# A graph-network layer with a mixture of experts: the general path at the end is entered by a two-way switch, announced ahead, in place of a conditional

## The chip, the cores and the metric

The kernel runs on one core of a Trainium2 chip. A core has five engines that run their own instruction streams: TensorE (PE; its weight loads are shown as PEld), VectorE (DVE), ScalarE (ACT), GpSimd (POOL) and SyncE (SP). DVE, ACT and PE compute; SP here only issues transfers (DMAs) and waits. Engines wait for one another, and for the landing of transfers, by semaphores. The metric is the device time of one execution in microseconds (us), as the median of several runs.

## The reference

There are 625 nodes with 1024 features and 20,000 edges of two types. Cut to what matters:

```python
def reference(x, src, dst, edge_type_2, ...):
    x = x + gnn(_layernorm(x))            # 1. graph layer
    x = x + ffn(_layernorm(x))            # 2. mixture of experts
    return x

def gnn(h):                               # NUM_REL = 2, D_FF = 286
    n = ln_weight * h * rsqrt(mean(h * h) + 1e-6)
    y = n @ W_root + conv_bias
    for r in range(2):                    # mean over the edges of type r into a node
        w = (edge_type == r)
        sums = segment_sum(n[src] @ W_rel[r] * w[:, None], dst)
        cnt = segment_sum(w, dst)
        y = y + sums / maximum(cnt, 1)[:, None]
    return h + elu(y) @ wo_weight

def ffn(x):                               # 8 experts, 2 of them for each token; 2 shared ones
    shared = mean over s of (gelu(x @ sW1[s] + sb1[s]) @ sW2[s] + sb2[s])
    gates = x @ rW + rb
    w = softmax of the two largest gates, zero elsewhere
    moe = sum over e of w[:, e] * (gelu(x @ W1[e] + b1[e]) @ W2[e] + b2[e])
    return shared + moe
```

## The kernel before

The program holds two complete versions of the computation. `sparse_kernel` is the fast one. It counts edges in windows and routes tokens to the experts in slots of fixed number, so it holds only if every edge fell into its window and the routed tokens fit into the slots. It notes in `flag`, one integer in on-chip memory, whether either was violated. `dense_kernel` is the general one, which holds for any input. `gnn_ffn_kernel` runs `sparse_kernel` first, then loads the flag into a register of each engine (L1467) and, if it is above zero, runs `dense_kernel` as well, which writes the output anew (`tc.If`, L1468). With the inputs measured here the flag says that nothing was violated, so the general path is jumped over: its instructions stand in each engine's stream between the branch and the common end.

The flag is made up in two places. `check` (L697, L698) counts the edges found; `slots`, near 160 us, adds the excess of the routing and writes `flag` (L1256, L1257).

The work of `sparse_kernel` runs over five tiles of 125 nodes. First come the graph layer's projections and aggregations, then the shared experts' first matrices (L1115), the routing (`route`, `slots`), the gathered tokens through the experts' two matrices (L1337, L1395), and a scatter of the results to a table in memory by GpSimd (L1403; the handles are kept in the list `sent`). The table is read back by transfers of SP into the tiles `gs`.

Last is the output loop, over the five tiles `d`. For each tile TensorE multiplies the shared experts' hidden values with their second matrices into `p_o` (L1450) and adds the biases (L1452), in pieces of 512 columns (for the last tile 512, 256 and 256). VectorE adds each piece to `x1` by `add` (L1426), in an order fixed by hand with `tc.issue_after`, which queues an instruction behind another on its engine without waiting for the other's end. `store` (L1434) sends a finished tile, or for the last tile a finished piece, to the output: SP sends the first 112 rows, ScalarE's queue the last 13.

After the branch each engine raises the semaphores that the general path would have raised (its instructions are put down to L1468), and SP waits there for the landing of the stores. Then the tile context ends (L1497): SP waits for all, and a barrier over the engines closes the program.

`mybir.EngineType` names the engines, `nc.values_load` loads a value from on-chip memory into a register, and `PARTS` holds the two row ranges of `store`.

## Time and profile before

| | us |
|---|---|
| runs | 310.52, 310.69, 311.41 |
| median | 310.69 |
| profiled execution | 312.2 |
| its span, first to last instruction | 310.0 |
| TensorE busy in the span | 297.6 |
| last matmul ends | 303.55 |
| last addition ends | 304.01 |

The profile comes from one execution. Its times count from the first instruction of the program. An engine name with a `q` (SPq, PEldq) is the engine's sequencer: register, branch, semaphore and DMA-issuing instructions, which are not counted as busy time. The granted clock of TensorE was 0.998 of full speed.

In a source view each line holds the kernel's line, the engine, the operation, the tiles it writes and reads, a count, the shortest, median and longest duration in ns, and the first and last start in us. In the DMA view a queue has its packets, megabytes and share of the 16 DMA engines' time; the queues with the kind `instruction` bring the engines' own code, and q1 and q10 carry the data transfers of SP and ScalarE.

### The profile page before, as it was taken

What the parts mean: (1) busy time and instruction counts of PE and PEld (TensorE: products, weight loads), DVE (VectorE), ACT (ScalarE), POOL (GpSimd) and SP (SyncE); (2) the same over time, 40 slices, a digit from 0 to 9 for tenths busy, and PEclk for the clock granted to TensorE, in tenths of its full rate; (3) what the DMA queues carried; (4) which work ended last, traced back from release to release, by engine and by line L of the source; (5) the groups of instructions that cost most, each with busy time, mean ns of one, the idle gap of its engine ahead of it and who ended that gap; (6) DMA issues with size and microseconds to landing.
All of it is one profiled execution on the core that took longest, in us unless ns stands there. A gap on an engine that the chain in (4) does not pass through costs nothing.

```text
span 310.0 us, 4844 instructions
## 1 busy us (share of the span) xinstructions
PE 297.6 (96%) x1693; PEld 200.9 (65%) x1693; DVE 180.7 (58%) x541; ACT 110.1 (36%) x248; POOL 46.7 (15%) x98
## 2 busy tenths in 40 slices
PE   8799999999999999999999999999999999999991
PEld 7577777887888763456777798877854334444451
DVE  4899999977879676873895032122214211256920
ACT  3456123432436245333424145456459421000000
POOL 9600000000000012431112032120002232200000
PEclk9999999999999999999999999999999999999999
DMA  7999900000000499999999843421047555579351
GB/s 235 306 317 401 406 31 0 3 0 2 0 0 2 126 345 303 388 390 388 319 342 408 349 147 127 137 76 62 0 135 305 218 209 200 201 285 374 154 161 45
DMA packets 27409, 61.18 MB, mean 197 GB/s; under 512 B 2175, under 2 KB 16006, under 8 KB 27374
## 3 DMA queue, kind: packets, MB, share of 16 engines
q1 hardware_dynamic: 21806, 43.77, 39.8%
q0 software_dynamic: 5280, 16.69, 14.9%
q10 hardware_dynamic: 294, 0.35, 0.5%
q8 instruction: 16, 0.26, 0.4%
q14 instruction: 13, 0.11, 0.1%
HBM read 42.76 MB, written 18.81 MB: 199 GB/s over the span
## 4 chain that ended last, share of the span: by engine, by line
PE 78%; DVE 14%; DMA 3%; ACT 1%; issue 1%; SPq 1%; ACTq 0%
PE p_h L1337 12%; PE p_yj L1395 12%; PE p_pr L880 11%; PE p_o L1450 11%; PE p_sh L1115 10%; PE p_y L941 5%; PE p_agg L898 4%; DMA xh<-in_x_dram 3%; PE p_x L1318 3%; DVE ohk L850 2%; PE p_t L787 2%; DVE ohs L847 2%; DVE ohs L846 2%; PE cnt L859 2%; PE p_y L945 1%; DVE ct L808 1%
## 5 line engine op out<-in xcount | busy, mean ns | idle before, releaser
L880 PE MATMUL p_pr<-wg,nT 128*125 128x286 f32 x240 | 61.9, 408 | 0.0
L880 PEld LDWEIGHTS p_pr<-wg,nT 128*125 128x125 f32 x240 | 43.4, 187 | 11.9 <-ACT nT L793 0.4
L1337 PE MATMUL p_h<-w1a,xsT 128*128 (+2 forms) x176 | 40.0, 380 | 0.0
L1395 PE MATMUL p_yj<-w2a,hjT 128*128 (+2 forms) x88 | 38.6, 594 | 0.0
L1450 PE MATMUL p_o<-sw,shT 128*125 128x512 f32 (+1 forms) x88 | 36.1, 553 | 0.0
L1115 PE MATMUL p_sh<-h2T,sw 128*128 128x313 f32 (+1 forms) x128 | 35.2, 428 | 0.0
L1337 PEld LDWEIGHTS p_h<-w1a,xsT 128*128 128x128 f32 (+2 forms) x176 | 28.7, 168 | 7.4 <-issue 0.5
L1115 PEld LDWEIGHTS p_sh<-h2T,sw 128*128 128x128 f32 x128 | 23.7, 189 | 8.6 <-issue 0.2
L1395 PEld LDWEIGHTS p_yj<-w2a,hjT 128*128 128x128 f32 (+2 forms) x88 | 14.4, 168 | 22.4 <-issue 22.1
L1450 PEld LDWEIGHTS p_o<-sw,shT 128*125 128x125 f32 x88 | 16.4, 187 | 16.9 <-issue 16.2
L1399 DVE COPY ys<-p_yj 128x512 f32<-128x512 f32 x15 | 10.4, 692 | 28.7 <-PE p_yj L1395 27.1
L1341 DVE COPY hj<-p_h 128x256 f32<-128x256 f32 x11 | 4.7, 425 | 31.1 <-PE p_h L1337 31.1
L850 DVE TENSOR_TENSOR ohk<-iotk,cols 125x512 f16<-125x512 f16 (+4 forms) x49 | 22.3, 455 | 0.0
L846 DVE TENSOR_TENSOR ohs<-iota,cols 125x512 f16<-125x512 f16 (+3 forms) x49 | 18.2, 372 | 6.5 <-PE cnt L859 6.5
L898 PE MATMUL p_agg<-P,CT 125*125 125x287 bf16 x150 | 20.4, 286 | 0.2 <-DVE P L888 0.2
L955 POOL DMA_DIRECT2D x1d<-xh x10 | 5.3, 533 | 101.6 <-DVE xh L948 101.2
L859 PE MATMUL cnt<-ohk,ohs 125*128 125x128 f16 x223 | 17.9, 219 | 2.8 <-DVE ohs L847 2.8
L859 PEld LDWEIGHTS <-ohs 125*128 125x128 f16 x223 | 14.6, 98 | 7.8 <-DVE ohs L847 4.2
L941 PE MATMUL p_y<-wo_t,eT 128*125 128x512 f32 x40 | 19.2, 603 | 0.0
L898 PEld LDWEIGHTS <-CT 125*125 125x125 bf16 x150 | 18.4, 136 | 0.1
L1403 POOL DMA_INDIRECT yt<-ys,row x11 | 10.8, 984 | 50.5 <-DVE ys L1399 50.5
L847 DVE TENSOR_TENSOR ohs<-ohs,cols 125x512 f16<-125x512 f16 (+3 forms) x49 | 18.1, 369 | 0.0
(295 smaller groups left out, 421.7 us busy)
## 6 DMA issues: line engine op xcount, KB each, us to landing
w1a<-in_L_ffn_W_dram SPq DMA_DIRECT2D x8, 1024.0 KB, 10.9
w2a<-in_L_ffn_W_dram SPq DMA_DIRECT2D x8, 1024.0 KB, 5.1
yt<-zero SPq DMA_DIRECT2D x2, 2560.0 KB
g<-yt SPq DMA_DIRECT2D x10, 512.0 KB, 7.7
sw<-in_L_ffn_sW_dram SPq DMA_DIRECT2D x4, 1024.0 KB, 5.5
x<-x1d SPq DMA_DIRECT2D x5, 500.0 KB
wg<-in_L_gnn_W_rel_dram SPq DMA_DIRECT2D x2, 1144.0 KB, 19.6
x1d<-xh POOLq DMA_DIRECT2D x5, 448.0 KB, 6.2
```

The source lines that it names most:

```text
L846: nc.vector.tensor_tensor(os, row[:, None].to_broadcast(shape), key, op=ALU.is_equal)
L847: nc.vector.tensor_tensor(os, os, both(VV_, 128)[1], op=ALU.mult)
L850: nc.vector.tensor_tensor(halves(oh_k[:, :g, :kn]), row[:, None].to_broadcast(shape), key, op=ALU.is_equal)
L859: nc.tensor.matmul(accs[w][:, : R * WD], oh_s[:, i, :], oh_k[:, i, (w - lo) * 128 : (w - lo + 1) * 128], start=first, stop=last)
L880: nc.tensor.matmul(p[:TP, :F], nT[:, k, m * TP : (m + 1) * TP], wg[:, k, r, :], start=(k == 0), stop=(k == KD - 1))
L898: nc.tensor.matmul(p[:TP, : F + 1], CT[:, m, at : at + TP], P[:, m, r, i], start=(m == 0 and i == 0), stop=(m == NT - 1 and i == 2))
L941: nc.tensor.matmul(ps[s][:TP, :], eT[:, k, :], wo_t[:, k, s * 512 : (s + 1) * 512], start=(k == 0), stop=False)
L1115: nc.tensor.matmul(p[:, : z - a], sw1[:, i, k, t * 128 : (t + 1) * 128], h2T[:, k, a:z], start=(k == 0), stop=(k == KD - 1))
L1337: nc.tensor.matmul(p[a:b, :H], xsT[j][:, k, a:b], w1m[j, a][:, 0, k, :] if a else w1a[:, bass.ds(e, 1), k, :], start=(k == 0), stop=(k == ...
L1395: made = nc.tensor.matmul(p[a:b], hjT[:, j, k, a:b], w2m[j, a, k][:, at] if a else w2a[:, bass.ds(e, 1), k, at], start=(k == 0), stop=(k = ...
L1403: sent.append(nc.gpsimd.indirect_dma_start(out=yt, out_offset=bass.IndirectOffsetOnAxis(ap=row[:, j : j + 1], axis=0), in_=y, in_offset=No ...
L1450: nc.tensor.matmul(p[:TP, :n], shT[:, i, k, own], sw2[:, i, k, at], start=(i == 0 and k == 0), stop=False)
```

## The change

The conditional becomes a switch over two arms. The flag is turned round: it is now 1 where nothing was violated and 0 otherwise (one more operation on VectorE), so it can be the index of the switch. Arm 0 is the general path; arm 1, the usual one, is empty and stands last. Each engine reaches its arm by a jump to a computed place. The flag is loaded before the output loop's code rather than behind it. `near_end` puts an announcement of the coming jump, with the index, into one engine's stream behind a given instruction: for SP and ScalarE behind the store of the last tile but one, for GpSimd behind the last scatter, for TensorE behind the last matmul of the last tile's first piece, and for VectorE behind the addition before that piece's. A usual arm ends with a jump of its own to the common end.

```diff
@@ -44,6 +44,7 @@
 NQ = NJ - NM2
+ENG = mybir.EngineType
 YB = 1024
@@ -1254,7 +1255,8 @@
         nc.vector.tensor_copy(flagf[:, 1:2], over[:1, 3:4])
-        nc.vector.tensor_tensor(flag, flagf[:, 0:1], flagf[:, 1:2], op=ALU.add)
+        nc.vector.tensor_tensor(flagf[:, 0:1], flagf[:, 0:1], flagf[:, 1:2], op=ALU.add)
+        nc.vector.tensor_scalar(flag, flagf[:, 0:1], 0.5, None, op0=ALU.is_lt)
         return named
@@ -1431,8 +1433,18 @@
     def store(d, at):
         for g, eng in zip(PARTS, (nc.sync, nc.scalar)):
-            eng.dma_start(out[d * TP + g.start : d * TP + g.stop, at], x1[g, d, at])
-
+            put = eng.dma_start(out[d * TP + g.start : d * TP + g.stop, at], x1[g, d, at])
+            if d == NT - 2:
+                near_end(ENG.SP if eng is nc.sync else ENG.Activation, put)
+
+
+    ok = nc.values_load(flag, min_val=0, max_val=1)
+
+    def near_end(engine, inst):
+        with tc.issue_after(inst.ins):
+            tc.switch_hint({engine: ok}, 2, "sparse")
+
+    near_end(ENG.Pool, sent[-1])
     banks = 0
     for d in range(NT):
@@ -1449,7 +1461,10 @@
                         nc.tensor.matmul(p[:TP, :n], shT[:, i, k, own], sw2[:, i, k, at],
                                          start=(i == 0 and k == 0), stop=False)
-                nc.tensor.matmul(p[:TP, :n], wT[:, own], b23[:, at], start=False, stop=True)
+                done = nc.tensor.matmul(p[:TP, :n], wT[:, own], b23[:, at], start=False, stop=True)
+            if d == NT - 1 and at.start == 0:
+                near_end(ENG.PE, done)
+                near_end(ENG.DVE, added[-1])
             add(x1[:, d, at], p[:TP, :n], 1.0 / NS, x1[:, d, at])
@@ -1457,16 +1472,17 @@
         if d < NT - 1:
             store(d, slice(0, D))
+    return ok
 
 
 def gnn_ffn_kernel(tc, *args):
     nc = tc.nc
     with tc.tile_pool(name="flags", bufs=1) as flags:
         flag = flags.tile([1, 1], I32, name="flag")
-        sparse_kernel(tc, flag, *args)
-        off = nc.values_load(flag, min_val=0, max_val=EC * 4 + 1)
-        with tc.If(off > 0):
-            dense_kernel(tc, *args)
+        ok = sparse_kernel(tc, flag, *args)
+        for arm in tc.Switch(ok, 2, hint="sparse"):
+            if arm == 0:
+                dense_kernel(tc, *args)
```

## The prediction, made before the changed kernel ran

> **What bounds the kernel now.** I read the profile's page first, then the chain of waits from 285 us on, then the source views of the flag's load (L1467), of the branch (L1468) and of the end of the tile context (L1497), then SP's waits and the DMA view of the last microseconds, since the change touches little ahead of them.

> ```profile
> PE 297.6 (96%) x1693; PEld 200.9 (65%) x1693; DVE 180.7 (58%) x541; ACT 110.1 (36%) x248; POOL 46.7 (15%) x98
> ```
> ```profile
> 303.57 0.02 issue
> 303.59 0.42 DVE x L1426
> ```
> TensorE runs without a gap up to 303.55 us, and the chain of real work ends with the last addition of L1426 at 304.01. The span is 310.0, so 6 us follow in which no engine computes. Whatever the change is worth is worth it there, unless it opens a hole in TensorE's stream before 303.55.

> ```profile
> L1467 PEldq TENSOR_LOAD <-flag x1: 320/320/320, 299.7 to 299.7; - x1
> L1467 DVEq TENSOR_LOAD <-flag x1: 542/542/542, 303.6 to 303.6; - x1
> L1467 ACTq TENSOR_LOAD <-flag x1: 819/819/819, 304.4 to 304.4; - x1
> ...
> L1468 SPq EVENT_SEMAPHORE  x8: 17/17/17, 307.7 to 308.3; - x8
> L1468 PEldq COMPARE_BRANCH  x1: 4067/4067/4067, 300.2 to 300.2; - x1
> L1468 DVEq COMPARE_BRANCH  x1: 72/72/72, 304.2 to 304.2; - x1
> L1468 PEldq EVENT_SEMAPHORE  x1: 51/51/51, 304.3 to 304.3; - x1
> L1468 SPq COMPARE_BRANCH  x1: 53/53/53, 304.4 to 304.4; - x1
> L1468 ACTq COMPARE_BRANCH  x1: 54/54/54, 305.3 to 305.3; - x1
> L1468 ACTq EVENT_SEMAPHORE  x1: 17/17/17, 305.8 to 305.8; - x1
> L1468 DVEq EVENT_SEMAPHORE  x1: 21/21/21, 307.4 to 307.4; - x1
> ```
> ```profile
> L1497 SPq EVENT_SEMAPHORE  x14: 17/28/28, 308.3 to 309.9; - x14
> ```
> ```profile
> SPq L1468 <- SPq L1468: 3.4, 2, 3.2
> ```
> ```profile
> q1 hardware_dynamic: 132, 0.12, 8.8%
> q8 instruction: 1, 0.02, 1.9%
> q14 instruction: 3, 0.02, 1.5%
> ```
> Each engine jumps over the general path. ACT is at its next instruction 0.41 us after its branch (305.38 to 305.79), DVE only after 3.07 us (304.29 to 307.36), and PE's branch itself lasts 4.07 us: those two wait for code that isn't there. SP branches at 304.46 and does its first semaphore at 307.67, but not for code alone: in the trace's semaphore records the last updates of the two final stores come at 307.652 (ACT's store) and 307.822 us (SP's), and SP passes the two waits at 307.668 and 307.839, 16 ns later each. So the landing of the last store ends the kernel, and 2.1 us of semaphores and barrier follow it (307.84 to 309.95).

> That landing is late for one reason that the DMA records show. The store's packets start at 304.85, and all but one DMA engine's share is through by 305.54. Updates up to 305.983 make up all but three; the others are at 306.480, 307.652 and 307.822. The last share (seven packets of 1,024 bytes from SP, one from ACT) starts at 306.47, just as a 16,384-byte packet of the instruction queue q8 ends (304.953 to 306.488), and is slowed by an 8,192-byte packet of q14 (306.426 to 306.919). So the last store queues behind instruction fetches. The 16,384-byte one starts 0.67 us after PE came out of its branch at 304.28; another packet of the same size (301.874 to 302.807) lies inside PE's 4.07 us. I read them as PE's demand and the next stretch of code that it asks for on arrival.

> **The change part by part.** *Flag.* DVE gets one 1x1 operation more near 160 us. Its neighbours last 0.13 to 0.14 us (L1256, L1257). It stands ahead of the chain that makes `tok` (L1234, 160.71), and the first gather starts at 161.16 and is used by PE at 177; PE has shared-expert matmuls (L1115) until then. At nothing; 0.14 us if that cover were gone.

> *Loads of the flag.* Five TENSOR_LOADs remain, moved ahead of the output loop's end. ACT's 0.82 and DVE's 0.54 leave the tail, but ACT was done at 305.9 and DVE at 307.5, before SP's landing waits: no gain by themselves. On PE the load of 0.32 us and the announcement now stand 36 instructions (two groups of 8+1 matmuls with their weights) ahead of the end. PE's sequencer is that far ahead: its load ran at 299.73 while those 36 were still to execute, so 3.8 us of matmuls cover it. If they didn't, PE would lose 0.3 to 0.8 us.

> *Announcements.* Each is some register operations (SP's FUSED_REGOPS took 0.19 us) and one hint. On SP and ACT they stand behind the store of tile 3 (293.75 us); behind them waits the store of 296.97, so 2.8 us of idle queue cover them. On DVE they follow the addition that ends at 294.32, with 1.9 us idle. On POOL they follow the last scatter at 268, with the barrier 36 us away. What a hint fetches moves among transfers that nobody waits for.

> *Entry.* A compare-and-branch becomes a computed jump: say 0.2 to 0.5 us of register work on SP (once to twice its FUSED_REGOPS and a branch of 0.05). SP would arrive near 305.2 rather than 304.9, and the landing can't come before 305.98: hidden. If all announcements hold, PE jumps at about 301 and its follow-up packet of 16,384 bytes falls near 302, under the last matmuls, not on the last store. DVE has no demand fetch; its follow-up packet comes about 0.6 us after its arrival (0.59 in this trace, 307.36 to 307.94), near 305, as do SP's and ACT's. These are 8,192 bytes each (0.31 to 0.49 us), and one may stand ahead of one engine's share.

> *Landing.* Bounds: 305.98, the last update that nothing delayed (gain 1.84 us), and 307.82 as now (0). I take 306.48, the update that is 0.5 late at present, since one small packet in the way is what remains: gain 1.34 us.

> *Exit.* The usual arm holds SP's eight waits and then a jump to the common end, which follows the landing, so it counts in full. A taken branch whose code is there costs from its end to the next instruction 0.14 (POOL, 268.90 to 269.04) to 0.41 us (ACT), and itself 0.05. I take 0.28, the middle, as neither engine is SP. From below it can't be under 0.05, the branch itself. If the code isn't there it costs 3.07 (DVE), priced under the rivals. [...]

> *Sum.* The profiled execution took 312.2 us, 2.2 of them outside its span. 312.2 - 1.34 + 0.28 = 311.14. The median of the three runs is 310.69, 1.5 lower than the profiled one, so the same 1.06 less gives 309.63. The case's own range is a gain of 0.5 to 1.8 us: 308.9 to 310.2.

> [...]

> **The rivals.** *1, the store still waits (no change).* The follow-up packets of DVE, SP and ACT all come on arrival, now within 304.8 to 305.6, when the store's own packets flow. Three of 0.31 to 0.49 behind one another are 0.9 to 1.5 us on one DMA engine, against the 1.5 + 0.5 of now. For it: the trace already shows two such packets and a fetch on one share. Against: two updates were late by different amounts, so not all packets go one way. Then the gain is 0.3 to 0.9, less the exit's 0.28: 310.0 to 310.7.

> *2, the exit is not there (slower).* The usual arm is a small island behind the general path's block, and the common end lies beyond it. If SP's exit jump fetches its code, that stands behind the landing: 306.48 + 0.51 for eight semaphores (308.345 less 307.839) + 0.05 + 3.07 = 310.1, where now L1497 starts at 308.35: +1.8 us, 312.4. It decides if SP's step from the exit to L1497 exceeds 1.3 us; below that the earlier landing pays for it. For it: DVE and PE miss when they jump today. Against: ACT, POOL and SP seem to find theirs, and the end code is short.

> *3, the change doesn't do what it says.* The announcement is dropped or comes to nothing, and SP misses at the entry: 304.9 + 3.07 = 308.0, then 0.51 and the exit's 0.28, 308.8 where it is 308.35 now: +0.4 us, 311.1.

> **How the numbers follow.** Forecast 0.65, rival 1 0.12, rival 2 0.13, rival 3 0.10. A measurement of this kernel can tell about 0.3%, 0.93 us, from no change: bounds 309.76 and 311.62. The forecast's range lies for three quarters below 309.76 (its centre 0.13 below, the landing bounded at 305.98 above): 0.49 faster, 0.16 within. Rival 1 is within; rival 2 is slower; rival 3 is split, as its +0.4 would be 1 us if ACT or DVE lag too: 0.05 each. So faster 0.49, within 0.33, slower 0.18. The range 308.9 to 311.5 takes in the forecast, rival 1 and most of rival 3, and leaves out rival 2 and some of the edges. The forecast's own: 308.9 to 310.2.

> **What would show it.** Right: PE's jump ends before 303 and no instruction packet of 16,384 bytes lies between 304 and 307; DVE's step after its jump falls from 3.07 to under 0.5 us; SP's first landing wait ends by 306.5; its exit step is under 0.5; the rest from L1497 on stays at 1.6 us (308.35 to 309.95). Wrong: PE's last matmul later than 303.55 by more than 0.3; an SP landing wait still near 307.7; or more than 1.3 us between SP's last semaphore of the arm and its first of L1497.

## The result: 314.2 us, slower by 1.1%, and the profile after

| | before | after |
|---|---|---|
| median of the runs taken together | 310.69 (5 runs, 310.52 to 311.41) | 314.21 (5 runs, 313.82 to 314.67) |
| ratio, 95% interval | | 1.011 [1.0093, 1.0128] |
| profiled execution, its span | 312.2, 310.0 | 314.21, 312.4 |
| last matmul ends | 303.55 | 303.07 |
| last matmul's end to the span's end | 6.40 | 9.35 |

The page's busy times and the chain of work say first what did not change. TensorE's busy time is 1.8 us longer than before (297.6), but that lies in the first 20 us (18.32 us busy there against 16.06); two later executions of the kernel before have 17.87 and 18.33.

```profile
PE 299.4 (96%) x1693; PEld 202.8 (65%) x1693; DVE 180.7 (58%) x542; ACT 110.2 (35%) x248; POOL 46.9 (15%) x98
```
```profile
303.10 0.42 DVE x L1428
```
From the last matmul of the edge counts (`cnt`, near 107 us) to the last output matmul TensorE takes 195.87 us, as before. So nothing was opened in its stream, and the whole loss lies behind the last matmul. The source view of the arms (L1483), where each engine's first instruction on arrival is a new announcement (of the way out), shows when each got there:

```profile
L1483 SPq EVENT_SEMAPHORE  x8: 17/17/17, 307.4 to 308.1; - x8
L1483 PEldq BRANCH_PREFETCH_HINT  x1: 36/36/36, 300.1 to 300.1; - x1
...
L1483 DVEq BRANCH_PREFETCH_HINT  x1: 45/45/45, 306.5 to 306.5; - x1
...
L1483 ACTq BRANCH_PREFETCH_HINT  x1: 36/36/36, 307.3 to 307.3; - x1
L1483 SPq BRANCH_PREFETCH_HINT  x1: 36/36/36, 307.3 to 307.3; - x1
```
The end of the context (L1513, before L1497) holds the jumps too, two for each engine: into the arm (first start) and out of it (last start).

```profile
L1513 SPq EVENT_SEMAPHORE  x14: 17/28/28, 310.7 to 312.4; - x14
...
L1513 PEldq COMPARE_BRANCH  x2: 361/2410/4459, 299.6 to 303.3; - x2
...
L1513 DVEq COMPARE_BRANCH  x2: 63/73/83, 303.3 to 306.7; - x2
...
L1513 SPq COMPARE_BRANCH  x2: 43/52/61, 304.1 to 308.1; - x2
L1513 ACTq COMPARE_BRANCH  x2: 43/52/62, 304.1 to 307.5; - x2
...
L1513 ACTq DRAIN  x2: 8/44/81, 311.5 to 311.8; - x2
```
Read together, from the end of a jump to the next instruction, and for PE, whose sequencer waits within the jump, the jump itself:

| engine | into the arm | out of the arm |
|---|---|---|
| PE | 0.36 us (299.63 to 299.99) | 4.46 (303.26 to 307.72) |
| DVE | 3.13 (303.42 to 306.55) | 4.34 (306.79 to 311.14) |
| ACT | 3.12 (304.19 to 307.31) | 4.00 (307.50 to 311.51) |
| SP | 3.15 (304.18 to 307.33) | 2.54 (308.18 to 310.72) |

The last DRAIN of ACT before the closing barrier ends at 311.59 us and SP's at 311.56, so these two chains end the kernel together. ACT's branch cost 0.41 us before. POOL's goes from 0.14 to 3.65 us, at 269 us, under TensorE's work, where it costs nothing. SP's wait in the arms and the DMA view of 303 to 309 us complete the picture:

```profile
SPq L1483 <- SPq L1483: 0.2, 1, 0.2
```
```profile
q14 instruction: 8, 0.07, 5.1%
q8 instruction: 2, 0.03, 3.2%
```
SP's wait for the landing has all but gone (3.4 us before, 0.2 now), but not because the store lands earlier. The last updates of the two final stores come at 307.42 and 307.62 us, 4.09 us after the last addition (3.81 before); SP merely comes later, at 307.33. Ten instruction packets lie in these six microseconds where there were four. In the DMA records the last share of the store (seven packets of 1,024 bytes from SP, one from ACT) starts at 306.36, just as the 16,384-byte packet of q8 ends (304.39 to 306.36); every other share had started by 305.60. That packet lies within TensorE's jump out of the arm (303.26 to 307.72), and q8's packets are read as TensorE's.

The balance is made against a usual execution of before (profiled twice below): its tail, from the last matmul's end to the span's end, is 5.31 and 5.48 us, say 5.4. After, the last store lands 1.3 us later behind the last addition (4.09 against 2.7 to 2.9), the way out adds 2.5, and the end from L1513 on takes 1.70 us (1.60 before): 3.9, as measured (9.35 - 5.4). What lies outside the span fell from 2.2 to 2.4 us to 1.8, some 0.45. So 3.9 - 0.45 = 3.5 us, the difference of the medians.

### The profile page after: what moved, and what is told of

It reads as the page before. It is cut to its first block, busy times and chain, and to the rows that moved or that the text cites. A ratio compares the mean times of both kernels' runs of the same rounds, so it can differ in the third digit from the quotient of the medians.

```text
span 312.4 us, 4901 instructions
## 1 busy us (share of the span) xinstructions
PE 299.4 (96%) x1693; PEld 202.8 (65%) x1693; DVE 180.7 (58%) x542; ACT 110.2 (35%) x248; POOL 46.9 (15%) x98
## 4 chain that ended last, share of the span: by engine, by line
PE 77%; DVE 14%; DMA 3%; ACT 1%; issue 1%; SPq 1%; ACTq 0%
PE p_h L1339 12%; PE p_yj L1397 12%; PE p_pr L881 11%; PE p_o L1462 11%; PE p_sh L1116 10%; PE p_y L942 5%; PE p_agg L899 4%; PE p_x L1320 3%; DMA xh<-in_x_dram 3%; DVE ohk L851 2%; PE p_t L788 2%; DVE ohs L848 2%; DVE ohs L847 2%; PE cnt L860 2%; PE p_y L946 1%; DVE ct L809 1%
## 5 line engine op out<-in xcount | busy, mean ns | idle before, releaser
L1312 POOL DMA_INDIRECT xs<-h2d,tok x11 | 11.3, 1027 | 45.6 <-PE p_x L1320 31.8
```

What stands on the lines that cost most here:

```text
L1312: nc.gpsimd.indirect_dma_start(out=xs, out_offset=None, in_=h2d, in_offset=bass.IndirectOffsetOnAxis(ap=tok[:, j : j + 1], axis=0))
```

## The experiments

**Theory A**, formed from this trace, where TensorE arrives at 299.99 us and a packet of q8 starts at 300.71, and where announcements 6 to 7 us ahead leave the entries of DVE, ACT and SP at 3.1 us and TensorE's at 0.36: an engine that runs into a new stretch of code asks at once for the next one, and an announcement only steers that request. Given before the engine's last request ahead of the jump, it brings the arm; given after it, it brings nothing. A jump whose code isn't there costs some 3 us and more, and its packets lie on the last store. **Rival B:** the announcements work, and the cost is in the switch's form (arms, computed jumps). **Rival C:** the extra instructions or the landing alone are the loss.

**Without any announcement.** The five `near_end` calls and the switch's `hint` argument are left out.

```diff
-            if d == NT - 2:
-                near_end(ENG.SP if eng is nc.sync else ENG.Activation, put)
...
-    near_end(ENG.Pool, sent[-1])
...
-            if d == NT - 1 and at.start == 0:
-                near_end(ENG.PE, done)
-                near_end(ENG.DVE, added[-1])
...
-        for arm in tc.Switch(ok, 2, hint="sparse"):
+        for arm in tc.Switch(ok, 2):
```

> The switch without any announcement. Theory A (an announcement fetches nothing by itself; it only steers the next fetch, which an engine makes when it runs into a new stretch of code, so on DVE, ACT and SP it came too late and did nothing): DVE, ACT and SP still wait 3.0 to 3.3 us at the entry, PE now waits about 4 us there too (from 299.6), SP's step out of the arm stays at 2.5 to 3.1 us, and the time stays within 0.6 us of the changed kernel's 314.2. Theory B (the announcements themselves are the cost, by register work or by fetches that collide): 312.5 or less. Theory C (they do help on all engines): 315.5 or more.

Measured: 315.47 us, ratio 1.0123 [1.0086, 1.0161]. The source view of its end code:

```profile
L1507 SPq EVENT_SEMAPHORE  x14: 17/28/28, 310.3 to 313.8; - x14
...
L1507 PEldq COMPARE_BRANCH  x2: 3832/4402/4972, 300.3 to 304.5; - x2
```
TensorE now waits twice, 3.83 us at the entry and 4.97 at the exit, and its last two fetches of 16,384 bytes take 2.76 and 1.60 us on top of the last store, which lands 5.40 us after the last addition. DVE, ACT and SP enter in 2.85, 3.74 and 2.93 us, no worse on the whole than with announcements. So of the five announcements TensorE's alone shortened an entry. In the DMA records the last share of the store starts at 307.68, as the longer of the two packets ends (307.69). The tail behind the last matmul is 10.41 us, 1.06 longer than with them; the intervals of the two ratios overlap, so 1.1 us is what the two profiles show. SP's way out cost only 0.38 us here; it had been in the arm for 2.4 us when it left.

**Announced early.** SP, ACT, DVE and POOL are told right after the flag is written (161 to 165 us), and their later announcements are left out; TensorE's stays in place.

```diff
+    ok = nc.values_load(flag, min_val=0, max_val=1)
+    tc.switch_hint({e: ok for e in (ENG.SP, ENG.Activation, ENG.DVE, ENG.Pool)}, 2, "sparse")
...
-            if d == NT - 2:
-                near_end(ENG.SP if eng is nc.sync else ENG.Activation, put)
...
-    near_end(ENG.Pool, sent[-1])
...
-                near_end(ENG.DVE, added[-1])
```

> The changed kernel with the announcements of DVE, ACT, SP and POOL moved to about 160 to 180 us, right behind the routing, and PE's left in place. Theory A: ACT runs into a new stretch of code near 234 us and DVE and SP near 280, after the announcement, so that fetch brings the usual arm: their entry falls from 3.1 to under 0.5 us, SP's landing waits end by 306.5, the step out of the arm stays at 2.5 to 3.1 us, and the time falls by 0.8 to 1.3 us to about 313.2. If the steered fetch takes the place of the next stretch and an engine still needs that, an extra wait of 3 us shows on that engine before 300 us. Rival (an announcement comes to nothing on these engines, wherever it stands): entries stay at 3.1 us and the time at 314.2.

Measured: 312.35 us, ratio 1.0029 [1.0010, 1.0048]. Its arms and its end:

```profile
L1479 DVEq BRANCH_PREFETCH_HINT  x1: 45/45/45, 305.0 to 305.0; - x1
...
L1479 SPq BRANCH_PREFETCH_HINT  x1: 36/36/36, 305.7 to 305.7; - x1
```
```profile
L1509 DVEq COMPARE_BRANCH  x2: 63/73/83, 304.4 to 305.2; - x2
...
L1509 SPq COMPARE_BRANCH  x2: 37/52/67, 305.2 to 308.7; - x2
```
The entries take 0.50 (DVE), 0.45 (SP) and 0.42 us (ACT) instead of 3.1: the same announcement, some 135 us earlier, works. It adds no packet: between 150 and 300 us there are eight of q14 in this kernel, in the changed one and in the one with no announcement. POOL still misses (2.57 us), which A does not explain. SP leaves in 0.37 us, 3 us after it came in, where 2.5 to 3.1 us had been expected again. ACT and DVE, which leave within 0.3 us of arriving, pay 3.6 and 3.8 us. TensorE's exit fetch (0.96 us, from 305.34) still meets the last store, and it lands 3.54 us after the last addition. The tail falls from 9.35 to 6.58 us, while TensorE's stretch from `cnt` to the last matmul is 0.26 us longer (196.13 against 195.87): 2.5 us together, as the ratios give it (1.0110 less 1.0029, of 310.7 us). So some 2.5 of the 3.5 us were announcements that came too late. Rival C, the extra instructions or the landing alone, falls with that and with the unchanged 195.87 us of TensorE. Rival B keeps what is left (ratio 1.0029, 0.9 us): with the entries mended, the second jump of the switch and TensorE's fetch for it remain.

**Arms exchanged.** The usual arm stands first, the flag turned to match (`is_gt`).

```diff
-        nc.vector.tensor_scalar(flag, flagf[:, 0:1], 0.5, None, op0=ALU.is_lt)
+        nc.vector.tensor_scalar(flag, flagf[:, 0:1], 0.5, None, op0=ALU.is_gt)
-            if arm == 0:
+            if arm == 1:
                 dense_kernel(tc, *args)
```

> The changed kernel with the two arms exchanged: the usual, empty arm stands first, right behind the jump, and the general path behind it. Theory A, with each arm starting on a stretch of code of its own: the entry is the next stretch, which the engines hold already, and costs under 0.5 us on all engines; the way out now leads over the general path and costs SP 2.5 to 3.1 us as before; the landing comes 0.5 to 1 us earlier, the time is 313 to 314. Rival (the end lies close behind an arm that stands last, and only the entry is at fault): the way out becomes costlier than in the changed kernel and the time is 315 or more.

Measured: 314.86 us, ratio 1.011 [1.0072, 1.0148]. In the source view of its end:

```profile
L1513 SPq EVENT_SEMAPHORE  x14: 17/28/28, 311.5 to 313.0; - x14
...
L1513 SPq COMPARE_BRANCH  x2: 43/55/67, 304.3 to 308.1; - x2
```
```profile
L1483 SPq BRANCH_PREFETCH_HINT  x1: 36/36/36, 304.8 to 304.8; - x1
```
Now every entry hits (0.36 to 0.50 us) and every exit misses (SP 3.31 us, TensorE 4.25). SP stays in the arm for 3.3 us, and yet its exit takes 3.31 (308.14 to 311.45): the arm that follows in the program, the general path, lies between it and the end. Its own announcement of the exit, given on arrival at 304.81, did not bring the end in that time. So what made the entries cheap here is the order of the program, and the announcement placed in the arm was too late or of no use. The time was expected at 313 to 314 with an earlier landing; it is no better than the changed kernel's, as the landing comes 3.89 us after the last addition (4.09 there) and SP's way out is dearer (3.31 against 2.54). In this order SP's one miss stands behind the landing.

**Announced between the two,** SP at 242 us, ACT at 266, DVE at 268, by the same call behind other instructions.

```diff
+    near_end(ENG.SP, loaded)
+    near_end(ENG.Activation, copied_a)
+    near_end(ENG.DVE, copied_v)
...
-            if d == NT - 2:
-                near_end(ENG.SP if eng is nc.sync else ENG.Activation, put)
...
-                near_end(ENG.DVE, added[-1])
```

> The changed kernel with the announcements of SP, ACT and DVE at about 235 to 267 us: SP's behind the loads of x1, ACT's and DVE's behind their last copies of the expert results. Theory A (an announcement only steers the next fetch, and that is made when an engine runs into a new stretch of code): ACT made its last such fetch near 234 us, DVE and SP make theirs near 280, so DVE and SP are at their arm in under 0.6 us after the jump and ACT still waits 3 us; SP leaves its arm in under 0.6 us, ACT's way out ends the program, and the time lies between the early announcements' 312.4 and the changed kernel's 314.2. Rival (early enough is enough, whatever the stretches): all three are there in under 0.6 us, time as with the early announcements. Rival (only announcements given by 165 us work): all three wait 3 us, 314.2.

Measured: 314.48 us, ratio 1.0124 [1.0083, 1.0164].

```profile
L1484 SPq BRANCH_PREFETCH_HINT  x1: 36/36/36, 304.9 to 304.9; - x1
L1484 DVEq BRANCH_PREFETCH_HINT  x1: 45/45/45, 306.8 to 306.8; - x1
```
```profile
L1514 SPq EVENT_SEMAPHORE  x14: 17/28/28, 308.1 to 312.7; - x14
...
L1514 ACTq DRAIN  x2: 8/44/80, 311.8 to 312.2; - x2
```
SP enters in 0.44 us, leaves in 0.37 and has nothing left to do by 308.96. DVE and ACT miss at the entry (3.07 and 3.24 us; DVE was expected to hit) and again at the exit (4.3 and 3.95), and the barrier waits for them until 311.8. Mending SP alone is worth nothing: SP, DVE and ACT each have a chain of two misses, and in the changed kernel those of DVE and ACT end within 0.5 us of SP's.

With DVE's miss theory A is not settled. Ahead of the jump, SP's announcement hit with 62 us here and with 144 when told early, ACT with 142 and DVE with 139; ACT missed with 39 us, DVE with 35, and all three with 6 to 7 us in the changed kernel. So a plain minimum lead (the time from the announcement to the jump), somewhere between 39 and 62 us, fits these three engines as well as "before the last request" does (POOL missed even with 108 us). No record says which engine a packet of q14 belongs to, so the last request of an engine, near 234 or 280 us in the expectations, is a reading. On TensorE 7 us were enough, and there the announcement may itself start the fetch: a packet of q8 starts 0.4 to 1.1 us behind it in all eight kernels that have one (293.81 behind 292.87 in the changed kernel), where the six without have theirs at 290.3 to 291.4. No run separates the two.

**No general path at all,** neither branch nor flag loads; and **the switch with one small transfer** in place of the general path.

The first is an edit of the kernel before, the second of the changed one.

```diff
         sparse_kernel(tc, flag, *args)
-        off = nc.values_load(flag, min_val=0, max_val=EC * 4 + 1)
-        with tc.If(off > 0):
-            dense_kernel(tc, *args)
```

> The kernel before with the general path, its branch and the loads of the flag left out (the output is the same for these inputs). It shows what the whole entry costs. Theory: the last store lands 1.9 us after the last addition as no code is fetched then, the eight semaphores behind the branch go, and the time is 308.2 to 309.2. Rival (SP's landing is not delayed by code): 309.8 or more.

```diff
-                dense_kernel(tc, *args)
+                nc.sync.dma_start(args[-1][0:1, 0:1], args[0][0:1, 0:1])
```

> The changed kernel with the general path left out: arm 0 holds a single small transfer in its place, so that both arms are a few instructions long (the output is the same for these inputs). Theory A with aligned arms (each arm and what follows lie on stretches of their own, whatever the length of the general path): SP, ACT and DVE still miss at the entry or at the way out, and the time is within 1 us of 314.2. Rival (the length of the jumped-over code is what counts): entry and way out take under 0.5 us each, the last store lands by 306.3, and the time is 309.0 to 310.0.

Measured: 309.16 us, ratio 0.9934 [0.9913, 0.9954], and 309.02, ratio 0.9931 [0.9913, 0.995]. In the second the whole switch stands in the middle of the output loop (TensorE's two jumps at 283 to 290 us), so for TensorE, SP, ACT and DVE it is no test of a jump's length. POOL's jump stands where it did, at 269 us, and there it is one: with arms of a few instructions POOL still takes 3.65 us to get in and 3.12 to get out. Both kernels show the same bound. With no code fetched at the end (no instruction queue in the DMA view of 303 to 309 us) the last store lands 1.9 us after the last addition, and the tail is 3.6 to 3.7 us. All that a general path costs before the change is thus about 0.7%, 2 us.

**Before, twice again.** The unchanged kernel, profiled twice.

> The kernel before, unchanged, profiled once more, because its first profiled execution (312.2) was 1.5 us above the median. If the late landing that the prediction built on (3.8 us after the last addition) is usual, it shows again and the span from the last matmul's end stays at 6.4 us; if it belonged to a slow execution, the landing comes 1.9 to 3 us after the last addition and that stretch is 4.5 to 5.6 us.

> The same again, for a third execution of the kernel before: 6.4 us from the last matmul's end to the end of the span if the late landing is usual, 4.5 to 5.6 us if not.

Measured: 311.08 and 310.57 us. The branch in the second:

```profile
L1468 SPq EVENT_SEMAPHORE  x8: 17/17/17, 305.9 to 306.6; - x8
L1468 PEldq COMPARE_BRANCH  x1: 3567/3567/3567, 299.5 to 299.5; - x1
```
The store lands 2.89 and 2.72 us after the last addition, where the execution that the prediction read had 3.81: that one was the latest of the three, and most of the 1.34 us that the forecast took at the landing was its own bad luck.

**Before with the last tile in pieces of 256, 512 and 256 columns,** to bring TensorE's fetch forward by half a piece.

```diff
-        for at in ((0, 512), (512, D)) if d < NT - 1 else ((0, 512), (512, 768), (768, D)):
+        for at in ((0, 512), (512, D)) if d < NT - 1 else ((0, 256), (256, 768), (768, D)):
```

> The kernel before, with its conditional, and the last tile's pieces of 256, 512 and 256 columns in place of 512, 256 and 256. If PE's sequencer runs two pieces ahead, its branch comes 1.8 us earlier (298.4), it is over by 302.6 and its follow-up packet of 16,384 bytes is through by 304.7, before the last store's packets: the last store lands 1.9 to 2.8 us after the last addition instead of 3.8, and the time is 309.3 to 309.9. Rival (the landing is late for another reason): 3.8 us stay, 310.5 to 311.

Measured: 310.63 us, ratio 0.9989 [0.9976, 1.0003]: no sure gain. TensorE's jump ends at 302.46 and its follow-up fetch comes at 303.75, the landing 2.55 us after the last addition, but the usual landing was not much later to begin with.

**The conditional kept, and announced.** Theory A says what to keep of the change: one jump, over the general path, whose target is the end itself, and an announcement before the engine's last fetch. First TensorE alone, behind the last matmul of the last tile's first piece; then VectorE too; that call stands behind the routing in the kernel, but the trace has it at the start of VectorE's stream.

```diff
+    tc.mark_branch_hint_location("general", "LikelyTaken", [mybir.EngineType.DVE])   # second kernel only
...
+            if d == NT - 1 and at.start == 0:
+                with tc.issue_after(done.ins):
+                    tc.mark_branch_hint_location("general", "LikelyTaken", [mybir.EngineType.PE])
-        with tc.If(off > 0):
+        with tc.If(off > 0, label="general"):
```

> The kernel before, with its If and its general path where they were; the only edit is an announcement of the branch's usual outcome to TensorE alone, behind the last matmul of the last output tile's first piece, eight matmuls ahead of the branch. Theory A (an announcement given before the engine's next instruction fetch steers that fetch, and TensorE's follow-up packet of 16,384 bytes then comes before the last stores instead of on them): TensorE's COMPARE_BRANCH step falls from 3.6 to 4.1 us to under 0.5, the last landing comes 1.9 to 2.5 us after the last addition instead of 2.7 to 2.9, and the time falls by 0.3 to 0.9 us: 309.8 to 310.8, ratio 0.997 to 0.999. Rival: TensorE's step falls, but VectorE's own fetches of 8,192 bytes still stand on the last store, or TensorE's announcement comes after its last fetch and does nothing: ratio 0.999 to 1.001. Other rival: the announced stretch is fetched in place of something that is needed, and the end's fetch comes later: ratio over 1.002.

> As v_if_hint_pe, and VectorE too has an announcement, at the start of its stream, ahead of its fetches. Theory A: VectorE's step at the branch falls from 3.07 us to 0.4 to 0.6 as well, its packets move away from the last stores, landing 1.9 to 2.2 us after the last addition, the time 0.8 to 1.5 us under the kernel before (309.2 to 310.0, ratio 0.995 to 0.9975), close to the 309.16 of the kernel without a general path. Rival: an announcement so early is overtaken by VectorE's later fetches (it has run through several stretches by then) and nothing differs from v_if_hint_pe.

Measured: 310.03 us, ratio 0.9959 [0.9944, 0.9974], and 309.77, ratio 0.9955 [0.9939, 0.9971], with 311.35 for the kernel before on the same chip. The source views of the branch, first with TensorE's announcement and then with both:

```profile
L1471 PEldq COMPARE_BRANCH  x1: 408/408/408, 300.2 to 300.2; - x1
...
L1471 DVEq COMPARE_BRANCH  x1: 72/72/72, 304.2 to 304.2; - x1
...
L1471 DVEq EVENT_SEMAPHORE  x1: 21/21/21, 307.4 to 307.4; - x1
```
```profile
L1472 SPq EVENT_SEMAPHORE  x8: 17/17/17, 305.3 to 306.0; - x8
L1472 PEldq COMPARE_BRANCH  x1: 408/408/408, 299.7 to 299.7; - x1
...
L1472 DVEq COMPARE_BRANCH  x1: 84/84/84, 303.7 to 303.7; - x1
...
L1472 DVEq EVENT_SEMAPHORE  x1: 21/21/21, 304.4 to 304.4; - x1
```
TensorE's jump falls from 3.6 to 4.1 us to 0.41, its follow-up packet starts at 301.25 and no packet of 16,384 bytes lies behind 303. VectorE's step, 3.09 us in the first, is 0.52 in the second. The last store lands 2.44 and 1.99 us after the last addition, and the tails are 5.03 and 4.58 us. The intervals of the two overlap, so what VectorE's part adds isn't settled. TensorE's alone gained more than expected (0.9959 where 0.997 to 0.999 stood); part is time outside the span, 1.8 us here against 2.2 to 2.4. Of the shortening of that part no run shows the cause.

Last, both announcements with the pieces of 256, 512 and 256:

> v_if_hint_pe_dve with the last output tile cut into pieces of 256, 512 and 256 columns instead of 512, 256 and 256, so that the wide middle store, not the first, is the next to last. What it tells: whether the announced kernel still has a wait in its tail that the order of the pieces sets. If its landing is already as short as the kernel's without a general path (1.9 us after the last addition), the order changes nothing: 309.5 to 310.0, tail behind the last matmul 4.5 to 4.7 us. If TensorE's announcement now comes at a worse place (its branch is announced four matmuls' columns earlier, ahead of another fetch), TensorE's step is 3.6 us again and the time 310.3 to 310.8. If the wide store late costs, the landing is later by 0.3 to 0.6 us: 310.0 to 310.4.

Measured: 309.70 us, ratio 0.9958 [0.9941, 0.9974] against 310.71 on its chip; tail 4.71 us, landing 2.1 us after the last addition. The order of the pieces changes nothing that can be told. These announced conditionals beat both kernels, by 0.4 to 0.45% and by about 1.5%.

## Why the prediction was wrong, step by step

**Exit: the step that failed.** It was taken at 0.28 us on the ground that ACT's, POOL's and SP's branches had found their code before. It measured 2.54 us on SP and 4.0 to 4.5 on ACT, DVE and PE. The rows of ACT and POOL that it rests on show a gap behind the branch (0.41 and 0.14 us); what fills it they don't show. And they came from another layout: there each of these engines has only its own part of the general path, whose length no run shows, between the branch and its target. In the switch even POOL misses at the entry, and it does so with a general path of one transfer too (3.65 us). So the layout of the switch, and not the length of what is jumped over, takes the code out of reach there; that each arm has a stretch of code of its own is the reading of it. And with the usual arm last, the exit was cheap only for an engine that had stayed in the arm long enough: SP after 2.4 us and more (0.37 to 0.38 us in three kernels), while after 0.84 us SP pays 2.54, and DVE and ACT, which leave after 0.2 to 0.3 us, pay 3.5 to 4.3. POOL stands between: 1.9 us in the arm and 1.45 and 1.29 at the exit (changed kernel, announced between the two), 2.0 to 2.4 us and 0.37 to 0.38 (no announcement, early). TensorE doesn't fit: it had been in the arm for 3.2 us and still paid 4.46. This is rival 2 in its place and sign. Its price, 312.4, was 1.8 us short: it had the landing 2.47 us after the last addition (306.48 less 304.01), which measured 4.09, and it was added to the late execution, which hid 1.0 more; against that SP's step was 0.5 shorter than its 3.07, and the time outside the span fell by 0.45.

**Announcements and Entry: failed.** "If all announcements hold" carried the forecast, and three of those that count at the end did not. The prediction costed what an announcement delays but never asked how far ahead it must stand. SP's came 7 us before its jump and fetched nothing. (The prediction also placed these announcements too early: the stores of tile 3 are those of 296.97 us, not of 293.75, and the addition before the last tile's first is that of 296.25. SP's, ACT's and DVE's ran at 296.8 to 298.1.) Between 280.9 and 300 us one instruction packet was fetched in all, q8's, and that is read as TensorE's, as it starts 0.94 us behind TensorE's announcement (293.81 behind 292.87):

```profile
q1 hardware_dynamic: 1135, 4.07, 58.0%
...
q8 instruction: 1, 0.02, 0.3%
```
No q14 line is there. SP reached the arm at 307.33, not 305.2, which is rival 3's entry (3.15 us where it put 3.07). By itself that cost SP nothing, as it still waited 0.2 us for the landing; it left SP only 0.84 us in the arm, too short for a cheap way out (2.54 us), and ACT and DVE entered as late. So the late announcements brought nothing that an entry shows (3.1 us and more), while TensorE's (0.36 us, 3.83 with none) and the early ones of SP, ACT and DVE (0.42 to 0.50) brought the target of the jump in time.

**Landing: wrong in sign, and mis-sized.** The gain of 1.34 us was to come from TensorE's fetch moving off the last store. The fetch of the entry did move (q8 at 300.71), as predicted. But TensorE must jump once more, after its last matmul, and the fetch read as that jump's (304.39 to 306.36, 16,384 bytes) falls where the old one fell (304.95 to 306.49); the last store landed at 307.62. That TensorE's second jump has a fetch of its own was overlooked. The mechanism itself holds: in three kernels the last share of the store starts as that packet ends (306.36 here, 307.68 with no announcement, 305.92 with those between the two; in the other two switches at the end no such edge stands out). Ordered by what is fetched at the end, with one profiled execution for each kernel but the one before, the landing comes 1.9 us after the last addition (nothing fetched), 2.0 to 2.4 (conditional announced), 2.5 to 2.9 (conditional, but for the one late execution), 3.4 to 4.1 (switch announced), 5.4 (switch not announced). Besides, the gain was measured from one late execution; from the usual landing 0.8 to 1.0 us were to be had, not 1.3 to 1.8. Taken off the median, 1.34 us put the landing 1.4 to 1.6 us after the last addition, earlier than with no code fetched at all.

**The miss in one sum.** From the forecast 309.63 to 314.21 are 4.6 us. They are, within 0.1 us, 2.3 for SP's exit (2.54 where 0.28 stood), 1.6 for the landing (4.09 where 2.47 stood), 1.0 for the late execution that the gain was read from, 0.1 for the end code, less 0.45 outside the span.

**Right:** the flag's operation, the loads and the announcements cost TensorE nothing (195.87 us in both); the end code takes 1.7 us (1.6 forecast); the last store queues behind instruction fetches (its last share starts at 306.36, as q8's packet ends); and the mark for "wrong", over 1.3 us between SP's last semaphore of the arm and its first of the end, was met with 2.64.

**Left open:** why POOL's early announcement missed; why TensorE's exit misses after 3.2 us in the arm, with a packet of 16,384 bytes fetched meanwhile (300.71 to 302.36); how early an announcement must stand, and whether an engine's last request or the lead decides it; which q14 packet belongs to which engine; why the time outside the span is 0.45 us shorter in all kernels but the plain conditional.

## What to carry to other kernels

Count the jumps that each engine makes behind the last piece of work, and ask for each how long the engine has been on that stretch of code (SP's exit cost 2.54 us after 0.84 us in the arm and 0.38 after 2.4, but TensorE's 4.46 after 3.2); two short hops in a row can cost two misses (DVE 3.13 and 4.34 us), where the one jump over the general path cost DVE one (3.07 us). Announce a coming jump early (here 62 us and more served SP, ACT and DVE, and under 40 us didn't; on TensorE 7 us were enough), not just ahead of the jump, and see in the trace that the step after the jump has become short (0.36 to 0.52 us here). Profile the kernel before more than once ahead of pricing a gain in its last microseconds.

## What was not expected of the hardware

An announcement can stand far ahead: VectorE's ran in the first microsecond of the program, and the step at the branch at 303.7 us was 0.52 us with it and 3.09 without.
